# One pass for the row maximum and the row factor in layer 1's softmax, and slots that return when a store has landed

## The chip, the cores and the metric

The kernel runs on one core of a Trainium2 chip. The metric is the device time of one execution in microseconds, as the median of several runs. The profile of a kernel is one execution, taken by the hardware profiler.

## What is computed

Two layers, each an attention and a feed-forward part. Every part is wrapped the same way: `x = x + LN(part(LN(x)))`. x is (2, 512, 512) in float32. Layer 0's attention is causal with 32 query heads and 8 key heads; layer 1's attention, where the change lies, has 32 heads of 128 and normalizes queries and keys by their root mean square:

```
q = rmsnorm(x @ Wq + bq, gq); k = rmsnorm(x @ Wk + bk, gk); v = x @ Wv + bv
scores = einsum('bnhd,bmhd->bhnm', q, k) / sqrt(128)
attn = softmax(scores)
out = einsum('bhnm,bmhd->bnhd', attn, v) @ Wo + bo
rmsnorm(x, w) = w * (x * rsqrt(mean(x*x) + 1e-6))
```

The feed-forward parts are a linear layer with low-rank additions (layer 0), and a gated one with 1376 hidden columns and low-rank additions (layer 1).

## The kernel before, in words

**Precision and tiles.** Products are kept near float32 by splitting each operand into a rounded high half and the rest, and adding three products (`mm3`, line 393). The high half is a rounding copy, mostly on ScalarE; the low half is a difference on GpSimd or VectorE. The 512 rows of each batch element are four tiles of 128 rows. Activations stay transposed in SBUF (`xh`, `xl`), the sums of a part in `y`.

**Units.** A layer's attention is cut into 16 head pairs for 2 batch elements, 32 units per layer. In layer 1 a unit projects K and Q (`proj`, line 1039), squares and sums them for the root mean square, and takes the power -0.5 on GpSimd; for K the factor is multiplied in, for Q it is kept as `rq`, one column for each tile and head (line 1084), and applied to the scores. K is multiplied by `g`, the product of the two weight vectors and 1/sqrt(128) (`consts`, line 429). In most units the transposes are made in 32x32 blocks on VectorE and put in place by a trip through DRAM (`flip`, line 1097, buffers kdk and kdq); in a layer's first and last units TensorE transposes.

**The scores.** `l1_score` (line 1169) issues, for each tile of 128 queries, three products of 512 columns into a PSUM bank, then on VectorE the negated row maximum `m` of the bank (line 1178), then the product `mr = m * r` with the row's factor r from `rq`, another VectorE instruction on 128x1. `softmax_tail` (line 681) follows: ScalarE takes `exp(r * s + mr)` from the bank and its row sums, VectorE the reciprocal, one of three engines multiplies the rows by it; then VectorE transposes blocks, DMA writes them to DRAM (pd) and reads them back in place, and each piece is split and used in the product with V (`av_items`, line 839). Layer 0's scores (`l0_score`, line 989) get their causal mask and row minimum in one VectorE pass over the bank, in place, and an exponential with scale -1 and bias m.

**The order of the work.** Python writes the program in the order of a plan that it makes while it runs. Every stage is a generator; `yield` hands the stage back to the planner until the planner's clocks say that what it has issued is done. `Engine.cost` (line 70) prices each instruction: on VectorE a 512-wide pass over PSUM at 512/960 + 0.07 us, the same for a row maximum and for a scaling; on ScalarE every row operand of the scale, the bias or the sum adds 0.093 us. `pick` (line 127) gives an operation to the engine that would be done first. `streams` (line 345) interleaves the units: scores and V products in main order, projections and output products as fills. Each engine executes its instructions in the order in which they were written, so the plan fixes each queue. All transfers are issued on SP's queue.

**Slots.** A tile is taken from a slot and given back with `rel` when its last reader is issued. The large tiles are halves of 37 shared slots; `NBUF` and `PHASES` (line 40) cap how many each kind may have. The hardware still makes the next writer of a slot wait for the reader.

**The residual.** `resid` (line 549) forms x + LN(y) for a tile; `store` (line 580) adds the row constant in a tile `xo` from the slots "A", writes it to DRAM (xd) on SP's queue and gives the slot back right there (line 590); the last level writes the output and gives back x in the same way (line 573).

Of the kernel before, what the change touches and what calls it, by code (L numbers as in the profile page):

```python
# [14 lines left out]
ALU = mybir.AluOpType  # L15
AX = mybir.AxisListType
# [40 lines left out]
class Item:  # L57
    """a piece of TensorE's work, to be issued when cond holds"""

# [4 lines left out]
class Engine:  # L64
    """An engine that keeps its order of issue, with a clock (us) of its work."""

# [57 lines left out]
class Engines:  # L124
    WEIGHT = dict(vector=1.0, scalar=0.5, gpsimd=0.0)

    def pick(self, *cands):
        """issue the one of the candidates (engine, op, args...) that is done first"""
        def score(x):
            e = getattr(self, x[0])  # L130
            kw = x[-1] if isinstance(x[-1], dict) else {}
            c = e.cost(x[1], [y for y in x[2:] if not isinstance(y, dict)], kw)
            t = max(e.free, e.k.now + LAT)
            for y in x[2:]:
                if isinstance(y, bass.AP) and y.space == PSUM:
                    t = max(t, e.k.banks.get(y.name, 0.0))
            return t + c * (1 + self.WEIGHT[x[0]])
        x = min(cands, key=score)
        kw = x[-1] if isinstance(x[-1], dict) else {}
        return getattr(getattr(self, x[0]), x[1])(*[y for y in x[2:] if not isinstance(y, dict)], **kw)  # L140
# [9 lines left out]
    def mul(self, out, a, s):  # L150
        """by a factor of each row"""
        self.pick(("gpsimd", "tensor_scalar", out, a, s, 1.0, ALU.mult, ALU.mult),
                  ("vector", "tensor_scalar", out, a, s, None, ALU.mult),
                  ("scalar", "activation", out, a, AF.Copy, dict(scale=s)))

    def copy(self, out, a):
        """from PSUM"""
        self.pick(("scalar", "copy", out, a), ("vector", "tensor_copy", out, a))
# [8 lines left out]
class Kern:  # L167
    """Work is written as items: functions, or generators that yield the time
    (of TensorE's work) after which their next stage is to be issued."""

# [30 lines left out]

# [1 line left out]
    def slot(self, tag):  # L203
# [12 lines left out]

    # the large tiles: a half or the whole of a slot each (halves of one type only in a slot)
    HALF = dict(W=2, Wk=1, nat=2, v=2, PT=2, TN=2, KT=2, raw=1, bb=1, bqk=1, qk=1, P=1, x=1, A=1, T=1, xn=1, pt=1, ot=1,
# [52 lines left out]

# [1 line left out]
    def step(self, g):  # L273
# [22 lines left out]
    def phase(self, i):  # L296
        """what is tuned for each phase of the work"""
        for k, v in PHASES[i].items():
            if k in self.NBUF:
                self.NBUF[k] = v  # L300
            elif k in self.nc.WEIGHT:
                self.nc.WEIGHT[k] = v
            else:
                setattr(self, k, v)
# [20 lines left out]
    def wait(self, tag, n=1):  # L325
        """in a stage: until n slots are free, first come first served"""
        q = self.queues.setdefault(tag, [])
        ticket = object()
        q.append(ticket)
        while q[0] is not ticket or not self.has(tag, n):  # L330
            yield 0.1
        q.pop(0)

    def low(self, eng):
        """in a stage of low priority: until the engine has nothing issued to it"""
        e = getattr(self.nc, eng)
        while e.free > self.now + 0.01:
            yield e.free - self.now
# [6 lines left out]
    def streams(self, main, fills, bg):  # L345
        """Issue the streams of items, each in its order: a fill when its nominal place in
        main has come, or main waits; bg starts at its nominal place."""
        mi = bi = idle = 0
# [27 lines left out]

# [1 line left out]
    def pe(self, t):  # L378
        """t: at the full clock, which TensorE has after a busy tick only"""
        s = max(self.clk, self.now)  # L380
# [12 lines left out]
    def mm3(self, out, pairs, start=True, stop=True):  # L393
        """exact hi/lo products: hi hi + hi lo + lo hi"""
        n = len(pairs)
# [8 lines left out]

# [1 line left out]
    def setup(self):  # L406
# [22 lines left out]
    def consts(self):  # L429
# [4 lines left out]
        yield  # L434
        nc.vector.scalar_tensor_tensor(self.g, self.gqk[:, 0:1], SCALE, self.gqk[:, 1:2], ALU.mult, ALU.mult)

# [3 lines left out]

# [1 line left out]
    def split(self, hi, lo, raw):  # L442
        """hi + lo = raw exactly"""
        nc = self.nc
# [33 lines left out]

# [1 line left out]
    def ln_stats(self, src):  # L480
# [68 lines left out]
    def resid(self, b, tt, lvl):  # L549
        """x of level lvl + 1 = x + LN(y); returned short of a constant of each row"""  # L550
        nc = self.nc
# [9 lines left out]
        if lvl == 3:  # L561
# [9 lines left out]
            yield  # L571
            nc.sync.dma_start(self.xsrc(b, tt, 4), x)
            self.rel(x)
            return
# [5 lines left out]
        def store():  # L580
# [5 lines left out]
            if lvl == 0:  # L586
                self.xin[b, tt, 1] = xo
                return
            nc.sync.dma_start(self.xsrc(b, tt, lvl + 1), xo)
            self.rel(xo)  # L590
        self.spawn(store)
        return x

    def boundary(self, b, tt, lvl):
        """from the finished y of level lvl on"""
        x = yield from self.resid(b, tt, lvl)
# [18 lines left out]

# [1 line left out]
    def out_proj(self, b, first, last, ot, w, badd, lvl):  # L617
        """y += O Wo over the heads of this unit"""
        def one(tt):
# [61 lines left out]
    def softmax_tail(self, st, j, qt, ps, bias, scale, w):  # L681
# [13 lines left out]
        if not st.get("lag"):  # L695
            st["p", j, qt] = pr
            return
        # P^T = 32 x 32 blocks transposed on VectorE, and the blocks put in place on their way through DRAM
        yield from self.wait("T")
# [60 lines left out]
    def unit_done(self, st):  # L760
        """after the last use of V"""
        if st["vlast"]:
            self.rel(*st["v"]["v"])
            if "v32" in st["v"]:
                self.rel(st["v"]["v32"])

    def pv_items(self, st, j, voff, causal, bias):
        """transposes of P, then O^T = V^T P^T, split"""
        box = {}
# [69 lines left out]
    def av_items(self, st, j, voff, bias):  # L839
        """O^T = V^T P^T by halves of the queries, split"""  # L840
        box = {}
# [41 lines left out]

# [1 line left out]
    def l0_init(self):  # L885
# [11 lines left out]
    def l0_zero(self):  # L897
        """the parts of pd0 that stay unused"""
        nc = self.nc
# [113 lines left out]

# [1 line left out]
    def l1_init(self):  # L1015
# [18 lines left out]
    def l1_pre(self, hp, b, w, lag):  # L1034
# [62 lines left out]
        def flip(n):  # L1097
            """the transposes as 32 x 32 blocks on VectorE, put in place on their way through DRAM"""
            nat = st["nat" + n]
# [69 lines left out]
    def l1_score(self, st, j):  # L1169
        def one(qt):  # L1170
# [4 lines left out]
            if qt == NT - 1:  # L1175
                self.rel(*st["q"][j], *st["k"][j])
            m = self.t("m", [P, 1])
            nc.vector.tensor_reduce(m, ps, AX.X, ALU.max, negate=True)
            yield
            while "rq" not in st:  # L1180
                yield 0.3
            r = st["rq"][:, 2 * qt + j:2 * qt + j + 1]
            mr = self.t("mr", [P, 1])
            nc.vector.tensor_tensor(mr, m, r, ALU.mult)
            yield
            self.rel(m)
            yield from self.softmax_tail(st, j, qt, ps, mr, r, S)
            if j and qt == NT - 1:
# [3 lines left out]

# [1 line left out]
    def f0_init(self):  # L1194
# [38 lines left out]

# [1 line left out]
    def f1_init(self):  # L1235
        """rows 0:16, 32:48, 64:80 of the pieces: hi of a low-rank factor, lo in block k; others 0"""
        nc, a = self.nc, self.a
# [150 lines left out]
    def f1_post(self, js, b, sts, last):  # L1388
        """y += g W2 over the chunks of units js"""
        def one(tt):  # L1390
# [29 lines left out]

# [1 line left out]
    def run(self, nu0=16, nu1=16, nf=6):  # L1422
        # at the ends of a layer's units some run batch by batch, each then with weights of its own
        units = []
# [17 lines left out]
        def pre(n):  # L1442
            """early, mid items and state of unit n"""
            if n not in sts:
# [43 lines left out]
        for k in FIRST.split():  # L1488
            for f in todo[k]:
                self.do(f)  # L1490
        # weights start this many units before (early, mid, late parts)
        bgs = {}
# [143 lines left out]
def _layout(i):  # L1636
    """Layouts of the arrays only: transposes and tilings."""
    n = {k: np.asarray(v) for k, v in i.items()}
# [44 lines left out]
```

## Time and profile before

| | us |
|---|---|
| median of 3 runs | 2111.77 (2107.32 to 2115.55) |
| span of the profiled execution | 2117.8 |
| TensorE busy | 2056.7 |
| VectorE busy | 1801.4 |
| GpSimd busy | 1446.3 |
| ScalarE busy | 1337.7 |

The span is the profiled execution's own time, from its first to its last instruction; it lies 0.3% above the median of the runs. In the lines below, PE is TensorE's products and PEld its weight loads, DVE is VectorE, ACT is ScalarE, POOL is GpSimd, SP the engine that issues transfers. A group names the tiles that are written and read (`m<-ps_s`), without their numbers: ps_s is a bank of scores, ps_pj of projections, ps_oy of V products and output products, ps_tr of transposes; `ar` is any large tile of the shared slots. Every instruction has line L102, since a helper records them all; groups are told apart by tiles and shapes. A number after a bar is busy time, then the mean duration of one in ns, then the idle time of the engine just before them and what ended it. "PEclk" is the granted clock of TensorE as a share of the full one.

Layer 1's attention begins at about 750 us (its first rq at 754.4) and its last exponential is issued at 1896.2.

### The profile page before, as it was taken

To read this page: it belongs to the slowest core of one execution; us is meant where nothing else is said; L and a number is where in the kernel's file an instruction comes from. 1 tells how busy PE (TensorE), PEld (TensorE's weight loads), DVE (VectorE), ACT (ScalarE), POOL (GpSimd) and SP (SyncE) were. 2 spreads that over 40 slices of the span, in tenths; PEclk is the share of its full clock that TensorE was granted. 3 is DMA by queue.
4 is the path that set the end of the run, shared out by engine and by line. 5 is a ranking of instruction groups with operands and counts; after the bars stand their busy time and mean duration, and the time that the engine had idled before them with its cause. 6 is when DMAs were issued, how large, how long until landed. Compare 5 with 4: busy or idle time off the path is not lost.

```text
span 2117.8 us, 41211 instructions
## 1 busy us (share of the span) xinstructions
PE 2056.7 (97%) x12605; PEld 1827.5 (86%) x12605; DVE 1801.4 (85%) x4210; ACT 1337.7 (63%) x3247; POOL 1446.3 (68%) x1786
## 2 busy tenths in 40 slices
PE   8999999999999999999999999999999999989998
PEld 7888888888888798889899999999999898977886
DVE  7998899899888889889889999899989988888534
ACT  5776677577766668776666666666667666664212
POOL 5686678688875567877677777777777776774212
PEclk9999999999999999999999999999999999999999
DMA  2476567577652235887877777777777787763021
GB/s 98 127 183 166 145 185 183 143 200 199 177 159 66 71 103 166 244 232 223 227 202 229 220 227 211 207 221 219 225 206 232 213 240 212 224 178 93 31 67 44
DMA packets 476566, 370.54 MB, mean 175 GB/s; under 512 B 117400, under 2 KB 424488, under 8 KB 476344
## 3 DMA queue, kind: packets, MB, share of 16 engines
q1 hardware_dynamic: 476344, 367.91, 60.9%
q8 instruction: 99, 1.62, 0.3%
q14 instruction: 123, 1.01, 0.2%
HBM read 232.12 MB, written 135.66 MB: 174 GB/s over the span
## 4 chain that ended last, share of the span: by engine, by line
PE 54%; DMA 12%; DVE 9%; SPq 3%; issue 2%; POOL 2%; ACT 2%; DVEq 0%; ACTq 0%; POOLq 0%
PE ps_pj L102 23%; PE ps_oy L102 19%; PE ps_s L102 10%; DVE ar L102 6%; SPq L102 3%; DMA pd<-ar 3%; DMA ar<-pd 2%; POOL ar L102 2%; DMA kdk<-ar 2%; ACT ar L102 2%; DMA ar<-kdq 2%; DMA kdq<-ar 2%; PE ps_tr L102 1%; DMA ar<-pc 1%; DVE m L102 1%
## 5 line engine op out<-in xcount | busy, mean ns | idle before, releaser
L102 POOL TENSOR_TENSOR ar<-ar,ar 128x256 fp32r<-128x256 f32 (+4 forms) x1223 | 1058.3, 887 | 456.6 <-ACT ar L102 333.6
L102 PE MATMUL ps_oy<-ar,ar 128*128 128x256 f32 (+2 forms) x4014 | 832.2, 342 | 28.7 <-DVE ar L102 14.0
L102 PEld LDWEIGHTS ps_oy<-ar,ar 128*128 128x128 f32 x4014 | 653.5, 190 | 133.1 <-DVE ar L102 22.5
L102 ACT CAST ar<-ar 128x256 fp32r<-128x256 f32 (+3 forms) x1166 | 531.5, 490 | 305.4 <-DMA ar<-pd 117.1
L102 PE MATMUL ps_pj<-ar,xh 128*128 128x256 f32 (+1 forms) x3392 | 635.2, 285 | 0.9 <-POOL ar L102 0.6
L102 PEld LDWEIGHTS ps_pj<-ar,xh 128*128 128x128 f32 x3392 | 536.0, 190 | 14.5 <-POOL ar L102 1.1
L102 PE MATMUL ps_pj<-ar,xl 128*128 128x256 f32 (+1 forms) x1696 | 482.9, 285 | 0.0
L102 DVE STREAM_TRANSPOSE ar<-ar 128x256 f32<-128x256 f32 (+3 forms) x688 | 347.9, 533 | 16.9 <-DMA pd<-ar 9.7
L102 DVE TENSOR_TENSOR ar<-ps_pj,ar 128x512 f32<-128x512 f32 (+2 forms) x448 | 305.4, 683 | 52.5 <-PE ps_pj L102 44.8
L102 PE MATMUL ps_s<-ar,ar 128*128 128x512 f32 (+2 forms) x1252 | 338.5, 376 | 8.6 <-DVE ar L102 4.7
L102 PEld LDWEIGHTS ps_pj<-ar,xl 128*128 128x128 f32 x1696 | 322.9, 190 | 2.1 <-DVE xl L102 0.7
L102 PE MATMUL ps_pj<-xh,ar 128*128 128x512 f32 x816 | 286.6, 399 | 0.7 <-ACT xh L102 0.7
L102 DVE TENSOR_TENSOR y<-ps_oy,y 128x512 f32<-128x512 f32 x272 | 184.8, 680 | 81.8 <-PE ps_oy L102 80.2
L102 PEld LDWEIGHTS ps_s<-ar,ar 128*128 128x128 f32 x1252 | 214.5, 189 | 44.0 <-DVE ar L102 12.6
L102 DVE TENSOR_TENSOR ar<-ar,ar 128x256 fp32r<-128x256 f32 (+5 forms) x328 | 207.9, 652 | 51.1 <-ACT ar L102 50.1
L102 ACT ACTIVATE ar<-ps_s,mr,rq 128x512 f32<-128x512 f32 x256 | 198.6, 777 | 46.7 <-DVE mr L102 36.9
L102 PEld LDWEIGHTS ps_pj<-xh,ar 128*128 128x128 f32 x816 | 154.0, 189 | 31.7 <-ACT xh L102 1.1
L102 DVE TENSOR_REDUCE m<-ps_s 128x1 f32<-128x512 f32 x256 | 170.9, 673 | 6.2 <-PE ps_s L102 5.0
L102 ACT ACTIVATE ar<-ar,ri 128x512 f32<-128x512 f32 (+3 forms) x245 | 149.6, 621 | 38.3 <-DVE ri L102 37.1
L102 POOL TENSOR_SCALAR ar<-ar,ri 128x512 f32<-128x512 f32 (+3 forms) x202 | 133.0, 661 | 54.3 <-DVE ri L102 48.9
L102 PE MATMUL ps_pj<-xl,ar 128*128 128x512 f32 (+1 forms) x408 | 161.2, 395 | 0.0
L102 ACT ACTIVATE ar<-ps_s,m 128x512 f32<-128x512 f32 (+3 forms) x256 | 133.8, 526 | 23.4 <-DVE m L102 14.8
(91 smaller groups left out, 2105.5 us busy)
## 6 DMA issues: line engine op xcount, KB each, us to landing
pd<-ar SPq DMA_DIRECT2D x240, 256.0 KB, 3.7
ar<-pd SPq DMA_DIRECT2D x480, 128.0 KB, 3.3
ar<-pc SPq DMA_DIRECT2D x200, 128.0 KB, 3.0
ar<-in_wq SPq DMA_DIRECT2D x86, 256.0 KB, 4.1
ar<-in_wo SPq DMA_DIRECT2D x86, 256.0 KB, 3.6
kdk<-ar SPq DMA_DIRECT2D x31, 512.0 KB, 4.8
ar<-kdk SPq DMA_DIRECT2D x124, 128.0 KB, 4.0
kdq<-ar SPq DMA_DIRECT2D x31, 512.0 KB, 5.1
```

What stands on the lines that cost most here:

```text
L102: r = self.k.tc.keep_in_program_order(f(*args, **kw))
```

## The change

In layer 1 the row maximum and its multiplication by the factor become one VectorE pass over the bank: it multiplies every score by the row's factor in place, and its accumulator output is the row's minimum. `g` gets a minus sign, so the bank holds negated scores and the minimum is the negated maximum. The exponential gets the constant scale -1 and the bias m, as in layer 0. The pass is written behind the wait for `rq`, which in the kernel before stood between the maximum and the product. The residual's slots are given back one stage later, when the planner has the store as landed. The rest of the diff removes comments.

```diff
@@ consts
-        nc.vector.scalar_tensor_tensor(self.g, self.gqk[:, 0:1], SCALE, self.gqk[:, 1:2], ALU.mult, ALU.mult)
+        nc.vector.scalar_tensor_tensor(self.g, self.gqk[:, 0:1], -SCALE, self.gqk[:, 1:2], ALU.mult, ALU.mult)
@@ resid, the last level
             nc.sync.dma_start(self.xsrc(b, tt, 4), x)
+            yield
             self.rel(x)
@@ resid, store
             nc.sync.dma_start(self.xsrc(b, tt, lvl + 1), xo)
+            yield
             self.rel(xo)
@@ l1_score
-            m = self.t("m", [P, 1])
-            nc.vector.tensor_reduce(m, ps, AX.X, ALU.max, negate=True)
-            yield
             while "rq" not in st:
                 yield 0.3
             r = st["rq"][:, 2 * qt + j:2 * qt + j + 1]
-            mr = self.t("mr", [P, 1])
-            nc.vector.tensor_tensor(mr, m, r, ALU.mult)
+            m = self.t("m", [P, 1])
+
+            nc.vector.tensor_scalar(ps, ps, r, 3.0e38, ALU.mult, ALU.min, accum_out=m)
             yield
-            self.rel(m)
-            yield from self.softmax_tail(st, j, qt, ps, mr, r, S)
+            yield from self.softmax_tail(st, j, qt, ps, m, -1.0, S)
```

## The prediction

> **What bounds the kernel now.** I read the page's busy line first, then the busy time by stage, then what TensorE waits for in each stage, then the groups of instructions with their shapes kept apart.
>
> The page:
>
> ```profile
> PE 2056.7 (97%) x12605; PEld 1827.5 (86%) x12605; DVE 1801.4 (85%) x4210; ACT 1337.7 (63%) x3247; POOL 1446.3 (68%) x1786
> ```
>
> TensorE is busy 97% of the span, VectorE 85%. A busy TensorE need not be TensorE at its pace, so I looked at the chain that ended last: twelve products of 256 columns take 1.42 us wherever they follow each other (0.118 us each), twelve of 512 take 2.78 (0.232 each), early, late and in the middle. That is its pace, and the change touches no product. Hence the stages (my cuts: layer 0; the way to layer 1; its first units; its steady part; its last units; the feed-forward):
>
> ```profile
> core 0: us, PE busy (x) PEld busy (x) DVE busy (x) ACT busy (x) POOL busy (x), PEclk, DMA share, GB/s
> 0.00:640.00 640.00, 624.18 (x3408) 543.35 (x3409) 559.71 (x1480) 435.02 (x1227) 469.28 (x570) 1.00 0.60 163
> 640.00:780.00 140.00, 136.50 (x809) 116.12 (x808) 120.67 (x302) 86.84 (x202) 81.98 (x120) 1.00 0.21 69
> 780.00:1100.00 320.00, 307.99 (x2064) 279.02 (x2064) 282.68 (x624) 227.97 (x511) 241.28 (x291) 0.99 0.75 217
> 1100.00:1700.00 600.00, 595.26 (x4184) 552.45 (x4183) 547.03 (x1213) 390.61 (x901) 448.90 (x544) 1.00 0.76 219
> 1700.00:1910.00 210.00, 195.76 (x1263) 177.11 (x1262) 177.31 (x396) 140.46 (x309) 150.55 (x187) 0.96 0.74 211
> 1910.00:2118.00 208.00, 197.00 (x884) 159.48 (x882) 114.01 (x199) 56.78 (x101) 54.28 (x75) 0.99 0.18 58
> ```
>
> The second number is the length, the third TensorE's busy time. In the steady part TensorE lacks 4.7 us of 600: nothing there can bring much. It lacks 12.0 us in the first units and 14.2 in the last, and there the granted clock dips too: 0.01 x 320 = 3.2 us and 0.04 x 210 = 8.4. Layer 1's attention thus has 15.2 + 4.7 + 22.6 = 42.5 us to give, all that this change can win there. What TensorE waits for, first in the steady part, then in the last units (us, times, longest):
>
> ```profile
> PE ps_s L102 <- DVE ar L102: 4.2, 13, 0.5
> PE ps_oy L102 <- DVE ar L102: 0.4, 1, 0.4
> ```
>
> ```profile
> PE ps_oy L102 <- POOL ar L102: 5.6, 8, 1.5
> PE ps_oy L102 <- DVE ar L102: 3.6, 3, 2.2
> PE ps_tr L102 <- ACT ar L102: 2.5, 2, 1.6
> PE ps_oy L102 <- ACT ar L102: 2.2, 3, 1.5
> ```
>
> In the steady part it is VectorE alone, by tenths of a us. At the end it is whichever engine prepares the split probabilities for the product with V: a long chain that the order of issue placed too close.
>
> **The change part by part.** The rows that price it (busy us, mean ns of one):
>
> ```profile
> L102 ACT ACTIVATE ar<-ps_s,mr,rq 128x512 f32<-128x512 f32 x256 | 198.6, 777 | 46.7 <-DVE mr L102 36.9 <-DVE ri L102 4.1 <-DVE ar L102 2.1
> L102 DVE TENSOR_REDUCE m<-ps_s 128x1 f32<-128x512 f32 x256 | 170.9, 673 | 6.2 <-PE ps_s L102 5.0
> L102 DVE TENSOR_TENSOR mr<-m,rq 128x1 f32<-128x1 f32 x256 | 92.2, 365 | 0.0
> L102 DVE CUSTOM_DVE_ANT_0 ps_s<-ps_s,ar 128x512 f32<-128x512 f32 x64 | 44.8, 700 | 0.7 <-PE ps_s L102 0.6
> L102 ACT ACTIVATE ar<-ps_s,m 128x512 f32<-128x512 f32 x64 | 43.9, 686 | 4.6 <-DVE m L102 4.6
> L102 DVE DVE_READ_ACCUMULATOR2_ANT m<- 128x1 f32 x256 | 35.1, 137 | 0.0
> ```
>
> *VectorE, removed:* 256 x (673 + 365) = 265.7 us. *Added:* 256 passes that read a bank of scores, write it back and leave a row minimum. No such form is in the trace. The nearest is layer 0's masked pass, same tile and shape, also in place: 700 ns, and 137 for the reading of its accumulator. Ends: one instruction without a read-out at 669 (the scaling by a row factor in SBUF, 128x512), and 853 + 137 (the slowest 512-wide row, a product-and-sum over SBUF). The sums are -94, -51.5 and -12 us; I take -51.5. None is a loss.
>
> [...] The row says 365 for the tiny product, with 107 to 2451 ns from fastest to slowest. [...] The trace's mean decides: it is what VectorE's queue lost. [...]
>
> *ScalarE:* the constant scale takes 777 to 686 ns: 256 x 91 = -23.3 us. The score's chain gets shorter by some 0.3 us.
>
> *What the order of issue moves* (both programs compared, counts by form): 18 of the 128x1024 multiplications by g go from GpSimd (1.19 us) to ScalarE (1.15); row factors 16 from GpSimd, 7 from VectorE to ScalarE; 36 of the 256-wide roundings from ScalarE to VectorE, 12 of the 512-wide back; 21 of the 256-wide differences to GpSimd, 27 of the 512-wide ones to VectorE. With their mean durations: VectorE -45 us in all, ScalarE +5, GpSimd -52. Layer 1's attention (780 to 1910) has VectorE busy 1007 of 1130 us, 89%; it becomes 85%. No engine becomes a bound. Products (12,473) and transfers (2,098) stay the same in number.
>
> *The steady part* stays at TensorE's pace; of its 4.7 us I give back a third, -1.5.
>
> *First and last units:* here the order counts. I counted, in both orders, TensorE's work (at 0.118 and 0.234 us a product) between a head's scores and the product with V that uses them. First units: before, 10 of 14 such distances are under 27 us (down to 19.0); after, 4 of 10 (down to 18.5). Last units: the shortest goes from 18.8 to 20.2; from scores to a transpose on TensorE from 6.4 to 9.2. In the steady part 31.3 becomes 28.4 in half the units: still long. So I give back half of the first units' 15.2 (-7.5) and somewhat under a quarter of the last units' 22.6 (-5).
>
> *Slots given back at landing:* xo (16 stores) and the output tiles (8) stay taken for the 2.0 to 6.5 us of a landing. Cover: 74 half slots, and other work on ScalarE. What it removes is seen: ScalarE waited 3.4 us in 3 places for such stores, off the path. Without cover a writer waits a landing, as it did. Zero; ends -3.4 and +6.5. Where they stand on SP's queue, loads follow them; none waits newly there. The sign in g: zero, one 128x1 instruction either way.
>
> *A new wait:* the pass needs the row factor, so VectorE may stand at it with everything queued behind: sums into y (which hold TensorE's banks), transposes, split differences. See the third case.
>
> Sum: -1.5 - 7.5 - 5 = -14 us of the profiled 2117.8 (its span; nothing beyond it is counted). The runs' median is 2111.77, 0.3% below; scaled, 2098.
>
> **The rivals.** *Hidden anyway:* VectorE isn't the bound, the steady part is full, and the stalls at both ends belong to the chain through DRAM (3.7 us out, 3.3 in), which the change leaves. Then only 1.5 us and some 2 at the ends are won: 2108. For it: DMA and TensorE carry most of the chain there. Against it: the distances that got longer.
>
> *Slower, by the row factor:* GpSimd makes it (1.65 us) once per unit of 35 us. Between it and its first reader lay at least 11.2 us of TensorE's work before; in the new order 6.3 at least, in many units. It decides once GpSimd runs more than 6 us behind. If TensorE then loses 1.5 us in each of 16 units, 24 us: 2136. Against it: GpSimd waits 333.6 us for ScalarE in total, so it is mostly early; no wait of VectorE for the factor is in the trace.
>
> *All recovered:* 42.5 us, 2069; no reason why every stall should go.
>
> **How the numbers follow.** Forecast (stalls at the ends shrink) 45%, around 2098, its own range 2086 to 2101; hidden 35%, 2102 to 2116; slower by the factor or an equally unlucky order 17%; more than forecast 3%. A measurement tells about 0.5%, 10.6 us, from no change: below 2101.2 is faster, above 2122.3 slower. The unknown pass (-94 to -12 on VectorE) moves the result by a few us through the same stalls. For 8 in 10 the range is 2082 to 2121.
>
> **What would show it.** The pass as two rows near 700 and 137 ns, no mr row, the exponential at 686; VectorE about 45 us less busy; TensorE's idle time between 780 and 1100 near 6 us and its clock dips fewer; the steady part's at 3 to 4. Wrong if VectorE waits at the pass for rq, if the pass costs over 1 us, or if TensorE's waits at ps_oy in the first or last units are no smaller.

## The result

| | median us | lowest to highest | runs |
|---|---|---|---|
| before | 2111.80 | 2107.32 to 2115.55 | 5 |
| after | 2120.33 | 2117.39 to 2127.33 | 5 |

The changed kernel takes 1.0052 times as long as the kernel before, with a 95% interval of 1.0031 to 1.0072: slower by about 11 us by the ratio (8.5 by the medians of the table). The forecast was 2098 us. The range given (2082 to 2121) just holds the median; its direction is the other one. Later ratios are all to the kernel before, run beside it on the same chip. That kernel's own median lies between 2107.8 and 2115.0 us in the five later sessions, so only ratios are compared. Between sessions a ratio can move by more than its interval: one kernel, run in two of them, gave 1.0015 and 1.0035. Differences of 0.1 or 0.2% between runs of different sessions are therefore read with care.

### The profile page after: what moved, and what is told of

Read it like the earlier page. It is cut to its first block, busy times and chain, and to the rows that moved or that the text cites. A ratio compares the mean times of both kernels' runs of the same rounds, so it can differ in the third digit from the quotient of the medians.

```text
span 2118.5 us, 41177 instructions
## 1 busy us (share of the span) xinstructions
PE 2055.8 (97%) x12605; PEld 1828.2 (86%) x12605; DVE 1760.9 (83%) x4236; ACT 1347.8 (64%) x3260; POOL 1408.0 (66%) x1747
## 5 line engine op out<-in xcount | busy, mean ns | idle before, releaser
L102 POOL TENSOR_TENSOR ar<-ar,ar 128x256 fp32r<-128x256 f32 (+3 forms) x1217 | 1041.7, 879 | 475.2 <-ACT ar L102 351.2
L102 ACT CAST ar<-ar 128x256 fp32r<-128x256 f32 (+2 forms) x1142 | 529.8, 494 | 277.3 <-PE ps_oy L102 78.8
L102 DVE STREAM_TRANSPOSE ar<-ar 128x256 f32<-128x256 f32 (+3 forms) x688 | 348.3, 534 | 14.9 <-DMA pd<-ar 8.6
L102 PE MATMUL ps_s<-ar,ar 128*128 128x512 f32 (+2 forms) x1304 | 345.2, 378 | 11.5 <-ACT ar L102 6.7
L102 ACT ACTIVATE ar<-ps_s,m 128x512 f32<-128x512 f32 (+3 forms) x512 | 309.7, 607 | 58.1 <-DVE ps_s L102 25.1
L102 PEld LDWEIGHTS ps_s<-ar,ar 128*128 128x128 f32 x1304 | 221.4, 189 | 48.7 <-ACT ar L102 10.9
L102 DVE TENSOR_TENSOR ar<-ar,ar 128x256 fp32r<-128x256 f32 (+5 forms) x334 | 217.1, 667 | 53.0 <-ACT ar L102 48.2
L102 DVE TENSOR_SCALAR_CACHE_REDUCE ps_s<-ps_s,rq 128x512 f32<-128x512 f32 x256 | 188.9, 743 | 9.6 <-PE ps_s L102 9.3
L102 ACT ACTIVATE ar<-ar,ri 128x512 f32<-128x512 f32 (+3 forms) x268 | 166.5, 632 | 46.5 <-DVE ri L102 45.7
L102 POOL TENSOR_SCALAR ar<-ar,ri 128x512 f32<-128x512 f32 (+3 forms) x186 | 125.5, 677 | 70.4 <-DVE ri L102 62.8
L102 DVE CUSTOM_DVE_ANT_0 ps_s<-ps_s,ar 128x512 f32<-128x512 f32 (+3 forms) x256 | 121.5, 488 | 4.5 <-PE ps_s L102 4.0
```

Source lines behind the costliest of these rows:

```text
L102: r = self.k.tc.keep_in_program_order(f(*args, **kw))
```

## The profile after

The busy line of the page answers to the one shown first for before:

```profile
PE 2055.8 (97%) x12605; PEld 1828.2 (86%) x12605; DVE 1760.9 (83%) x4236; ACT 1347.8 (64%) x3260; POOL 1408.0 (66%) x1747
```

VectorE lost 40.5 us of work, as forecast to within 5. ScalarE gained 10 us (forecast: 5), though its exponentials became cheaper (777 to 687 ns), and GpSimd lost 38 (forecast: 52). The relief of VectorE was real; part of it went to ScalarE, to which the new plan hands more work.

The rows of the new softmax, with shapes kept apart (busy us, mean ns of one, then idle time before them and what ended it):

```profile
L102 DVE TENSOR_SCALAR_CACHE_REDUCE ps_s<-ps_s,rq 128x512 f32<-128x512 f32 x256 | 188.9, 743 | 9.6 <-PE ps_s L102 9.3
L102 DVE DVE_READ_ACCUMULATOR ps_s<-ps_s,rq 128x1 f32 x256 | 35.3, 138 | 0.0
L102 ACT ACTIVATE ar<-ps_s,m 128x512 f32<-128x512 f32 x320 | 219.6, 687 | 39.3 <-DVE ps_s L102 25.1 <-DVE ri L102 6.4 <-DVE m L102 3.9
```

The pass costs 743 + 138 = 881 ns where 673 + 365 = 1038 stood. What it waits for is the scores (9.3 of 9.6 us), not `rq`. The exponential is at 687. So each instruction did what it was meant to do.

The busy time by stage, in the same cuts:

```profile
core 0: us, PE busy (x) PEld busy (x) DVE busy (x) ACT busy (x) POOL busy (x), PEclk, DMA share, GB/s
0.00:640.00 640.00, 627.84 (x3424) 546.64 (x3425) 562.31 (x1487) 437.00 (x1232) 470.84 (x571) 1.00 0.60 163
640.00:780.00 140.00, 136.75 (x809) 116.26 (x808) 120.28 (x303) 88.14 (x203) 84.64 (x124) 1.00 0.22 71
780.00:1100.00 320.00, 307.09 (x2077) 280.96 (x2076) 272.76 (x636) 223.96 (x509) 234.37 (x280) 0.98 0.76 219
1100.00:1700.00 600.00, 597.20 (x4200) 554.71 (x4199) 518.31 (x1225) 407.14 (x921) 419.64 (x520) 1.00 0.75 220
1700.00:1910.00 210.00, 193.17 (x1239) 172.60 (x1239) 178.49 (x396) 136.60 (x301) 145.46 (x179) 0.97 0.72 206
1910.00:2118.00 208.00, 193.76 (x865) 157.03 (x864) 108.75 (x193) 55.01 (x97) 53.02 (x76) 0.98 0.17 55
```

TensorE's idle time in the first units is 12.9 us (12.0 before): nothing given back there. In the steady part it is 2.8 (4.7). In the last two stages it rose, from 14.2 to 16.8 and from 11.0 to 14.2. The two profiled spans (2117.8 and 2118.5) hide the loss: layer 0, whose code is the same, had done 3408 products by 640 us in the one execution and 3424 in the other. A single execution of this kernel moves by several us, so the stages only say where to look; the verdicts below come from timed runs.

What TensorE waits for in the changed kernel's last stage, and below it the same in the kernel before (us in total, times, longest):

```profile
PE ps_tr L102 <- ACT ar L102: 4.0, 2, 2.2
PE ps_oy L102 <- DVE ar L102: 1.1, 1, 1.1
```

```profile
PE ps_tr L102 <- ACT ar L102: 0.6, 1, 0.6
PE ps_oy L102 <- DVE ar L102: 0.5, 1, 0.5
```

Two waits of about 2 us stand where 0.6 stood. They are at the transposes of the layer norm, on the passage from layer 1's attention to the feed-forward, a place that the prediction did not look at.

## Experiments

The runs are numbered e1 to e18, in the order in which their expectations stand; every ratio is from five rounds, with 5 to 22 executions of the kernel named.

### Instructions and order taken apart

The plan is made from the planner's prices, so the two can be separated. In the first run the planner charges its clocks for the instructions that were removed while the new ones are written:

```diff
+            nc.vector.tensor_scalar(ps, ps, r, 3.0e38, ALU.mult, ALU.min, accum_out=mn)
+            yield
...
+            v.free = max(v.free, self.now + LAT) + 1 / 960 + 0.07
...
+            yield from self.softmax_tail(st, j, qt, ps, mn, -1.0, S, 0.093)
```

By the traces, TensorE's, GpSimd's and SP's queues are then those of before, instruction by instruction, and VectorE's and ScalarE's too but for the replaced ones. The second run does the reverse, in the changed kernel's queues: maximum and product are written, but charged as the one pass, with ScalarE charged 0.093 us less.

> Layer 1's new instructions (one pass, constant scale) in the order of issue of the kernel before: the planner is charged for the removed instruction and for the dearer exponential, so that TensorE's, GpSimd's and SP's queues are those of before, instruction by instruction, and VectorE's and ScalarE's too but for the replaced ones. Theory ORDER (the new instructions are cheaper and the new order of issue loses more than they win): 2103 to 2110 us, 2 to 8 us below the kernel before. Theory INSTRUCTION (the pass in place, or its wait for the row factor, costs TensorE time): 2117 to 2123, like the changed kernel.

> The converse: the row maximum, the product with the factor and the exponential with two row operands, in the order of issue of the changed kernel (the planner is charged as for the one pass). Theory ORDER: 2120 to 2130, no faster than the changed kernel and slower than before. Theory INSTRUCTION: about 2112, like before.

Measured: new instructions in the old order 0.9985 (0.9974 to 0.9997), in a repetition on another chip 0.9992 (0.9981 to 1.0003, told below); old instructions in the new order 1.0134 (1.0114 to 1.0155). So the instructions are worth a little, 0.1%, in the old order, and 0.8% in the new one (1.0134 to 1.0052); and the new order costs 0.6% with the new instructions (1.0052 less 0.9989, the mean of the two), 1.3% with the old. The 0.8 and the 0.6% compare runs of two sessions, but they are three times what the repetition of one kernel moved, or more. The order is what loses. For the old instructions it loses more than the 2120 to 2130 us that ORDER expected (1.0134 of 2112 is 2140).

### Which part of the diff changes the order

The third run has only the score part of the diff, the fourth only the two `yield`s ahead of `rel(x)` and `rel(xo)`.

> The score's part of the change alone, planned freely; the residual's slots are given back as before. If the score's part makes the loss: 2116 to 2124. If the slots do: 2100 to 2112. By theory ORDER any free plan may land anywhere within some 10 us of before, so that score part and slot part need not add up to the whole.

> The residual's slots given back at the landing, alone; the scores as before. Its instructions are those of before, only in another order. If only instructions matter: 2112, no difference. Theory ORDER: a difference of 3 to 10 us from before, of either sign, though nothing that runs has changed.

Measured: scores only 1.0043 (1.0031 to 1.0055), slots only 0.9995 (0.9983 to 1.0007). Alone, the slots do nothing: by the traces every engine keeps its order of instructions, so the difference of 3 to 10 us that ORDER expected for e4 had no ground. Together with the score's part they do change the plan. TensorE's queue in e3 is the changed kernel's for its first 11,598 of 12,605 instructions and then another, in which this is all that TensorE waits for from 1910 us on:

```profile
PE ps_oy L102 <- DVE ar L102: 0.2, 1, 0.2
```

The two waits of 2 us are not there, and e3 is still slower than the kernel before by 0.43%. So they cannot be all of the loss.

### The passage to the feed-forward

Layer 1's last 24 output products finish the rows of the last batch element. Before a row tile can be transposed for the feed-forward, it goes through the sum into y, the row statistics, the factor and a second layer norm, over VectorE, GpSimd and ScalarE. In the kernel before, two feed-forward blocks of 12 products (into ps_s and ps_pj) come behind the 24; in the changed kernel they come ahead of them. The expectations below speak of the blocks as lying between the last products into `ps_oy`; by the traces they lie behind layer 1's output products, among the feed-forward's own products into `ps_oy`.

TensorE's timeline of the kernel before, without the lines of the two blocks, which fill 1938.6 to 1941.4 and 1944.7 to 1947.5 (start, us, instructions, then idle time and its releaser in brackets):

```profile
1931.69 7.11 PE L102 MATMUL ps_oy<-ar,ar 128*128 128x512 f32 x30
...
1941.42 1.54 PE L102 MATMUL ps_oy<-ar,ar 128*128 128x512 f32 x6
1942.80 0.64 PE L102 MATMUL ps_tr<-ar,ar 96*128 96x256 f32 x4
1943.28 1.58 PE L102 MATMUL ps_oy<-ar,ar 128*128 128x512 f32 x6
...
1947.45 1.54 PE L102 MATMUL ps_oy<-ar,ar 128*128 128x512 f32 x6
1949.61 0.66 PE L102 MATMUL ps_tr<-ident,ar 128*128 128x128 f32 x4 [0.62 <-ACT ar L102]
```

And of the changed kernel, complete:

```profile
1933.25 9.92 PE L102 MATMUL ps_oy<-ar,ar 128*128 128x512 f32 x42
1943.01 0.64 PE L102 MATMUL ps_tr<-ar,ar 96*128 96x256 f32 x4
1943.48 2.96 PE L102 MATMUL ps_oy<-ar,ar 128*128 128x512 f32 x12
1948.67 0.66 PE L102 MATMUL ps_tr<-ident,ar 128*128 128x128 f32 x4 [2.23 <-ACT ar L102]
1951.13 1.12 PE L102 MATMUL ps_tr<-ident,ar 128*128 128x128 f32 x4 [1.80 <-ACT ar L102]
1951.89 4.01 PE L102 MATMUL ps_oy<-ar,ar 128*128 128x512 f32 x12
```

The sum of the first row tile starts on VectorE at 1933.27 in the first and at 1934.84 in the second. From there to the transposes with `ident` it is 16.3 and 13.8 us, and TensorE has work for 15.7 and for 11.6 of them. The chain is not slower in the changed kernel; it has lost its cover, the work that TensorE has meanwhile. A second cost follows: the last twelve products take 4.01 us where twelve take 2.96 three rows above. The granted clock of the changed kernel says why:

```profile
core 0: us, PE busy (x) PEld busy (x) DVE busy (x) ACT busy (x) POOL busy (x), PEclk, DMA share, GB/s
1940.00:1950.00 10.00, 7.09 (x34) 5.39 (x32) 9.68 (x23) 3.72 (x6) 5.26 (x11) 1.00 0.20 79
1950.00:1960.00 10.00, 8.87 (x39) 7.43 (x40) 6.96 (x15) 5.20 (x9) 4.79 (x8) 0.83 0.08 29
```

VectorE is busy 9.68 of 10 us in the stretch with the first hole, which suggests that the chain can hardly go faster there; in the next stretch the clock is 0.83, worth 1.7 us of 10. With the 4.0 us of waits that is some 6 us.

The fifth run mends only this: in the changed kernel the two blocks are held until one and two row tiles have their last output products issued, which puts them where they were before. The sixth spoils it in the kernel before: the output products are held until nine blocks are issued.

```diff
 # the changed kernel, blocks behind            (f1_pre)
-Item(lambda n=n: ok(n), ...)
+Item(lambda n=n: ok(n) and self.lp >= {7: 1, 8: 2}.get(self.ff, 0), ...)
 # the kernel before, blocks ahead              (run, post(NA - 1))
+y.cond = lambda ok=y.cond: ok() and self.ff >= 9
```

Here `ff` counts the blocks issued and `lp` the row tiles whose last output products are issued. Away from this place TensorE's queue stays as it was.

> The changed kernel, with one edit to its plan: the last two feed-forward blocks of 12 products that it issued ahead of layer 1's last output products are held until one and two of those output products are issued, which is the order of the kernel before at this place; all else of the plan stays. Theory BOUNDARY (the changed kernel loses at the passage from layer 1's attention to the feed-forward, since its last output products run back to back and the layer norm of their rows has nothing left to hide behind): TensorE's waits at ps_tr for ScalarE from 1910 us on go from 4.0 to under 1.5 us, and the time falls by 4 to 8 us, to some 2114 (ratio to the kernel before 1.0000 to 1.0033). Rival PLAN ELSEWHERE (the loss sits in the stages of layer 1's attention, whose order differs too): the time stays within 2 us of the changed kernel, ratio 1.004 to 1.007.

> The kernel before with the opposite edit: its last output products of layer 1 are held until nine feed-forward blocks are issued, so that they run back to back as in the changed kernel; instructions of the same kinds, all else of the plan stays. Theory BOUNDARY: slower than the kernel before by 4 to 8 us (ratio 1.002 to 1.004), with new waits of TensorE at ps_tr for ScalarE of 3 to 5 us after 1910. Rival PLAN ELSEWHERE: within 2 us, ratio 0.999 to 1.001.

Measured: changed kernel with the blocks behind 1.0017 (1.0007 to 1.0027), 0.35% less than without (measured in another session); kernel before with the blocks ahead 1.0028 (1.0018 to 1.0037), 0.28% more. In the traces, the two waits at ps_tr for ScalarE come to 0.7 us in the first, and to 4.0 in the second. Both directions agree: the passage costs 6 to 7 us. The traces say so too. TensorE's last 783 instructions are the same set in these four kernels and take 176.5 us in the kernel before, 183.3 in e6, 181.1 in the changed kernel and 177.4 in e5. The rival PLAN ELSEWHERE falls for this part, but not as a whole: 1.0017 is still 0.3% above 0.9989.

### Other plans

Two more plans of the changed kernel: K's multiplication by g fixed on GpSimd (which the changed plan had moved to ScalarE, 18 times), and another planner constant.

```diff
-                nc.mul(kt, kt, self.g)
+                nc.gpsimd.tensor_scalar(kt, kt, self.g, 1.0, ALU.mult, ALU.mult)
 # the other run
-LAT = 0.1
+LAT = 0.12
```

> The changed kernel with K's multiplication by g fixed on GpSimd, where nearly all of it stood in the kernel before, instead of left to the planner's choice (which moved 18 of them to ScalarE). The plan made around it differs in layer 1, keeps the two feed-forward blocks between the last output products, and has the longest distances of all between scores and V product. BOUNDARY: 2103 to 2112, near the new instructions in the order of before (2109). Rival LUCKY PLAN (the plan of the kernel before is well matched to the chip as a whole and any new one loses some 10 us somewhere): 2117 to 2128.

> The changed kernel with the planner's constant for the latency from one engine to the next at 0.12 us instead of 0.10: the same instructions in another plan, which like the changed kernel runs the last output products back to back (shortest distances from output product to the transposes of its rows 7.0 to 12.5 us of TensorE's work). BOUNDARY: 2116 to 2128, as slow as the changed kernel or slower. If it comes below 2112, back-to-back output products do not decide.

Measured: g on GpSimd 1.0041 (1.0028 to 1.0054), constant 0.12 1.0070 (1.0049 to 1.0091). The second is as BOUNDARY expected, but says little: its queue leaves the others' at TensorE's 155th instruction, in layer 0, and it waits 11.3 us in the steady part as well. The first is a miss for BOUNDARY and lies where LUCKY PLAN put it. With the blocks behind and the longest distances that I had counted, it still loses 0.5% against 0.9989. So the passage is not all, distances between scores and V product do not foretell the time, and the 18 multiplications on ScalarE are not the whole cause either.

### Where the rest lies

A plan is made forward in time, so one can be changed from a given tile of scores on. Ahead of each tile the planner's pricing is chosen by the number of tiles issued, 256 in all; the instructions are the new ones throughout. The expectations call e10 "new plan later" and e13 "new plan steady only".

```diff
+            self.sc = getattr(self, "sc", 0) + 1
+            if self.sc <= 48:      # e10; > 48 in e9; not in range(49, 177) in e13;
+                ...                # <= 208 in e14; <= 192 in e15: priced as the removed instructions
+            else:
+                ...                # priced as the changed kernel does
```

> The new instructions throughout. For the first 48 of layer 1's 256 tiles of scores the planner prices them as the changed kernel does, for the other 208 as the removed ones: TensorE's queue is that of the changed kernel up to 45% of its instructions, and that of the new instructions in the order of before over its last 55%. What is left of the changed kernel's loss once the passage to the feed-forward is mended is 0.32% (1.0017 against 0.9985). FIRST UNITS (this rest was lost in the first units): ratio near 1.0017. LATER (it was lost in the steady part and the last units): near 0.9985, as the new instructions in the order of before. In shares: in between.

> The new instructions throughout, the other way round: the first 48 tiles of scores priced as the removed ones, the rest as in the changed kernel. TensorE's queue is that of the order of before up to 45%, then a plan close to the changed kernel's, with the last output products back to back (42 in a row). FIRST UNITS: 0.9985 plus 0.0035 for the passage, 1.002. LATER: as the changed kernel, 1.005.

> The kernel of the run ahead of this one, with the two feed-forward blocks held until one and two of the last output products are issued. BOUNDARY, confirmed a second time if this is 0.0025 to 0.0035 below that run. FIRST UNITS: 0.9985, all of the loss undone. LATER: 1.0017.

> The new instructions in the order of before, a second time, as the yardstick for the three runs beside it on the same chip: 0.9974 to 0.9997 if the first measurement (0.9985) holds, at or above 1.0000 if its gain was chance.

> The new instructions throughout; the planner prices tiles of scores 49 to 176 of 256 as the changed kernel does, and all others as the removed instructions. TensorE's queue is that of the order of before in its first 45% and its last 19%, and that of the plan of the run new plan later in between, up to 76%. STEADY (the rest of the loss, some 0.3 to 0.45%, is lost in the steady part, by many small waits): ratio 1.001 to 1.004. LAST UNITS (it is lost after the steady part): 0.998 to 1.000, as the new instructions in the order of before. The trace should say the same: in the stages after 1000 us the scores' products come later by some 6 us in all (STEADY) or not at all.

> The new instructions throughout; the planner prices the first 208 tiles of scores as the removed instructions, and the last 48 as the changed kernel does: TensorE's queue is that of the order of before in its first 83%. At the passage to the feed-forward this plan keeps the two blocks between the last output products (30, block, 6, block). STEADY: 0.998 to 1.000. LAST UNITS: 1.001 to 1.004.

> As the run ahead of this one, but with the first 192 tiles priced as the removed instructions, 64 as in the changed kernel: TensorE's queue is that of the order of before in its first 79%, and here the plan runs the last 42 output products back to back. BOUNDARY: slower than the run ahead of it by 0.13 to 0.35%, with waits of TensorE at ps_tr for ScalarE of some 4 us at the passage; if the two are equal, the passage alone costs nothing.

| new plan in | ratio | 95% interval |
|---|---|---|
| nowhere (e1) | 0.9985 | 0.9974 to 0.9997 |
| nowhere, again (e12) | 0.9992 | 0.9981 to 1.0003 |
| first units (e9) | 0.9987 | 0.9978 to 0.9997 |
| steady part (e13) | 1.0015 | 1.0003 to 1.0026 |
| steady part, again (e18, told below) | 1.0035 | 1.0025 to 1.0045 |
| last units, blocks behind (e14) | 0.9987 | 0.9978 to 0.9996 |
| last units, blocks ahead (e15) | 1.0031 | 1.0021 to 1.0042 |
| all from the steady part on, blocks ahead (e10) | 1.0049 | 1.0032 to 1.0067 |
| the same, blocks behind (e11) | 1.0036 | 1.0022 to 1.0050 |
| everywhere (the changed kernel) | 1.0052 | 1.0031 to 1.0072 |

The first units and the last units, taken alone, neither lose nor gain. The steady part loses 0.26% and, in the repetition, 0.46% against 0.9989: 0.36% in the mean, some 7.6 us. The repetition, 1.0035, lies outside the 1.0003 to 1.0026 expected of it; only its sign repeats. The passage costs 0.13 to 0.44% in its four pairs (e11 to e10, before to e6, e5 to after, e14 to e15). The smallest of them, 0.13%, is below the 0.25 that BOUNDARY expected at least, and its intervals overlap; the largest is above the 0.35 expected at most and also has 16 more tiles in the new plan. e11 itself, at 1.0036, missed the 1.0017 that LATER gave it. With the mean of the four, 0.30%, the sum is 0.36 + 0.30 = 0.66%, and 0.63% are to be explained (1.0052 less 0.9989). That the two meet so closely is luck: the shares are uncertain by 0.1% or more, and e3 loses 0.43% without the passage.

The traces of single executions point the same way. TensorE's instructions 5,727 to 10,255 are the same set in all kernels named here. In the order of before they take 646.0 to 651.9 us (e1, e9, e12, e14), in the new plan 658.3 and 655.9 (e13, e18), some 8 us more; e13 had expected some 6.

Where the steady part loses is not to be seen at one place. TensorE's waits from 1000 to 1600 us with the new plan in the steady part (e13), and below in the order of before with the same instructions (e12):

```profile
PE ps_s L102 <- ACT ar L102: 3.7, 6, 1.5
PE ps_s L102 <- DVE ar L102: 2.0, 3, 1.2
PE ps_s L102 <- POOL ar L102: 1.8, 3, 1.0
PE ps_oy L102 <- DVE ar L102: 1.7, 2, 1.5
```

```profile
PE ps_s L102 <- DVE ar L102: 2.1, 7, 0.5
PE ps_oy L102 <- DVE ar L102: 0.7, 1, 0.7
```

9.2 us of waits stand against 2.8, but this sum does not part the two orders: it is 5.5 in e1, the same program as e12, 6.4 in the kernel before and 6.0 in the changed one. What is new is the scores' wait for ScalarE. With the order of before it is at most 0.4 us in any run, with the new plans told so far 1.8 to 6.6 (e8, with 0.3, is the exception). ScalarE's rounding copies of 512 columns, from 1000 to 1600 us, show what it waited for itself, again in e13 and then in e12:

```profile
L102 ACT CAST ar<-ar 128x512 fp32r<-128x512 f32 x132 | 80.0, 616 | 32.9 <-DMA ar<-kdq 14.7 <-DMA ar<-in_wv 6.1 <-DMA ar<-in_wo 4.2
```

```profile
L102 ACT CAST ar<-ar 128x512 fp32r<-128x512 f32 x126 | 74.3, 616 | 9.1 <-DMA ar<-in_wo 4.5 <-DVE ar L102 2.1 <-DMA ar<-kdq 1.2
```

14.7 us of idle time were ended by Q's blocks coming back from DRAM (`kdq`), against 1.2. One case of e13's timeline, ScalarE and then TensorE:

```profile
1434.32 0.62 ACT L102 CAST ar<-ar 128x512 fp32r<-128x512 f32 x1 [2.25 <-DMA ar<-kdq]
```

```profile
1434.99 1.91 PE L102 MATMUL ps_s<-ar,ar 128*128 128x512 f32 x6 [0.81 <-ACT ar L102]
```

The loads of these blocks are issued from 1428.71 on; the high half of Q is made the moment that they have landed, and the scores start the moment that it is made. A load takes 3.8 us from issue to landing in the median, and 3.7 in e12: it is not slower, it is issued too close ahead of its scores. ScalarE is not overloaded there, it waits. The same number parts all kernels told so far. With the order of before in the steady part these copies wait for kdq 0.9 to 1.5 us (3.7 in the slots-only kernel, under 1.1 in e14); with the new ones told so far it is 11.4 to 20.1 (13.9 in the changed kernel, 20.1 with g on GpSimd).

That is an agreement of traces. Two of three last runs try it (the third repeats e13): in the plan, Q's blocks are taken as landed later than before, so that more work goes between their loads and their scores.

```diff
 # flip, behind the four loads
             yield
+            if n == "q" and 48 < getattr(self, "sc", 0) <= 176:   # e16; in e17 1.5 and no upper end
+                yield 1.0
             if n == "k":
```

> The kernel of the run new plan steady only, with one edit: from tile of scores 49 to 176 the planner takes Q's blocks as landed 1.0 us later than it did, so that it puts more work between their loads from DRAM and the scores that use them. TensorE's first 45% and last 21% are again those of the order of before. Theory Q LATE (the steady part loses because Q's blocks come back from DRAM too close ahead of their scores): ScalarE's idle time ended by kdq in its 512-wide copies from 1000 to 1600 us falls from 14.7 to under 5, TensorE's waits there from 9.2 to some 4, and the ratio from 1.0015 to 0.999. Rival ANY NEW ORDER (the late blocks are a by-product): the kdq idle time falls, the ratio stays at 1.001 to 1.002.

> The kernel of the run new plan later with blocks between, with 1.5 us more for Q's blocks from tile 49 to the end: the changed kernel's prices in the steady and the last units, both faults mended. Q LATE: 0.998 to 1.000, against 1.0036 without this edit. ANY NEW ORDER: 1.002 to 1.005.

> The run new plan steady only a second time, as the yardstick beside the two others on the same chip: 1.0003 to 1.0026 if its first measurement (1.0015) holds; at 0.999 if the steady part's loss was chance.

Measured: e16 0.9995 (0.9984 to 1.0006), e18 beside it 1.0035 (1.0025 to 1.0045), e17 1.0067 (1.0052 to 1.0083). ScalarE's copies and then TensorE's waits of e16, 1000 to 1600 us:

```profile
L102 ACT CAST ar<-ar 128x512 fp32r<-128x512 f32 x136 | 82.9, 617 | 31.3 <-DMA ar<-in_wv 11.7 <-DMA ar<-kdq 5.3 <-PE ps_pj L102 4.2
```

```profile
PE ps_s L102 <- POOL ar L102: 2.8, 4, 0.9
PE ps_oy L102 <- DVE ar L102: 1.9, 2, 1.6
PE ps_oy L102 <- POOL ar L102: 0.5, 2, 0.4
PE ps_s L102 <- DVE ar L102: 0.4, 1, 0.4
PE ps_s L102 <- ACT ar L102: 0.3, 1, 0.3
```

The wait for kdq fell from 14.7 (14.9 in e18) to 5.3, the scores' wait for ScalarE from 3.7 to 0.3, and the time by 0.40% against e18, beside it on the same chip. The waits in all fell to 5.9 us, not to the 4 expected. One price in the plan, 1 us more, takes the steady part's loss away: instructions 5,727 to 10,255 take 651.3 us, as in the order of before. It does so without going back to that order, from which TensorE's queue in e16 differs in 392 places (in e13, 316). Weights that come late are not what e13 lost by: ScalarE's wait for them (in_wv) rose from 6.1 to 11.7 us. In this plan, then, Q LATE holds. But the edit also draws a new plan for the whole steady part, and e17 is a miss for both theories, above the 1.005 of ANY NEW ORDER. There kdq is down to 5.0 too, and yet TensorE waits more from 1000 to 1600 us than in e13, 10.9 us, now mostly for VectorE and GpSimd (its lines have L103, since the helper stands one line further down):

```profile
PE ps_oy L103 <- DVE ar L103: 5.7, 5, 1.4
PE ps_s L103 <- POOL ar L103: 4.7, 6, 1.5
```

In the last units TensorE lacks 19.4 us of 210 from 1700 to 1910 (16.8 in the changed kernel), at a clock of 0.95. So late Q blocks are one way for a plan to lose in the steady part, the one that e13 shows; that they are all of the changed kernel's loss there is not shown. Mending one fault of a plan draws a new plan behind it.

At the passage, e14 and e15 repeat what the changed kernel showed. In e14 the wait at these transposes is 0.65 us. In e15:

```profile
1928.19 9.95 PE L102 MATMUL ps_oy<-ar,ar 128*128 128x512 f32 x42
...
1943.61 0.66 PE L102 MATMUL ps_tr<-ident,ar 128*128 128x128 f32 x4 [2.20 <-ACT ar L102]
1946.08 1.12 PE L102 MATMUL ps_tr<-ident,ar 128*128 128x128 f32 x4 [1.81 <-ACT ar L102]
1946.84 5.45 PE L102 MATMUL ps_oy<-ar,ar 128*128 128x512 f32 x12
```

The clock in e15 is 0.77 from 1940 to 1950 and 0.89 in the next 10 us, in e14 1.00 in both.

A part of the losses is the clock's. In the timed runs its mean is 0.9942 to 0.9947 for the kernel before in every later session, 0.9943 in e16, 0.9935 in e18, 0.9920 in the changed kernel and 0.9896 in e2. As an estimate, 0.0025 of 2118 us is 5 of the changed kernel's 11 us. At its passage this is seen: the two waits cost their own 4.0 us, and from within the second one on the clock was half for 3.41 us (last section).

The best versions are the new instructions in an order close to that of before: e1, e9 and e14, each about 0.1% under the kernel before, some 2 to 3 us. The repetition e12, at 0.9992, has an interval that reaches 1.0003, so this gain is small and barely shown.

## Why the prediction was wrong

**The bound** held: TensorE is busy 97% of the span in the kernel before, in the changed kernel and in e1, and 96% in e2, and no other engine became one.

**The pass** was taken at 700 + 137 and measured 743 + 138, within its bounds. The instructions alone were put at -51.5 us; by the rows they are 256 x (881 - 1038) = -40, and with the order held VectorE is busy 31 us less (1801.4 to 1770.2 in e1). With the new order the -45 came out as -40.5. To take the tiny product at its mean in the trace, 365 ns, though its fastest took 107, was right for VectorE's time: in e2, which has it still, its mean was 346. What makes it so long was not shown.

**ScalarE's** 91 ns per exponential are there (777 to 687; 1337.7 to 1314.8 us in e1). That the order of issue hands it more than this, +5 in all, was forecast; it became +10.

**The steady part** (-1.5) was a miss in sign. With the order held nothing is lost there; in the new plan of e13 it costs 5.5 to 9.7 us (0.26 and 0.46%), which goes when Q's trip through DRAM is planned 1 us longer (e16). I had named transfers through DRAM only in a rival, for both ends, as something that the change leaves alone. I had also reasoned that it runs at TensorE's pace and cannot move much, which bounds what can be won there but not what can be lost.

**First and last units** (-7.5 and -5, nearly all of the forecast gain) are the steps that failed. They rested on two distances in the order, scores to V product and scores to transposes, which grew. Taken alone, the new plan in the first units brings nothing against the same instructions in the old order (0.9987 against 0.9989), and neither does that in the last units (0.9987). So these distances, as counted, are not what sets the time of these stages. The signs named for them did not come: TensorE's idle time from 780 to 1100 us is 12.9 us, not near 6, and its clock 0.98, not above 0.99. I had not counted a third distance, from a row tile's last output product to the transposes of its layer norm: for the first row tile of the last batch element it fell from 15.7 to 11.6 us of TensorE's work. It was in the compared orders to be read, and is worth the 6 to 7 us of e5 and e6. So the sum failed where it took gains in these units from a longer cover, and where it put the losses of a new order, 13 us in all, at nothing.

**The slots** at zero: right when alone (0.9995). With the score's part they move the plan of the passage, which the zero did not think of. **The wait for the row factor**: right to be set aside; no wait of VectorE for it is in the trace after.

**The rivals.** "Hidden anyway" had the instructions right: it put their worth at 3.5 us, and in the order of before they bring 2 to 3. "Slower" happened, but not by the row factor: by what its case called an equally unlucky order, which was named without a place or a price. The sum gave the order credit for gains and no debit.

## What to carry to other kernels

Where a planner or scheduler makes the order, a cheaper instruction is two changes: its own time, which here was worth 2 to 3 us, and a new order everywhere behind it, which here cost 13. Take them apart by letting the planner charge the old prices for the new instructions, and keep the old order if it is the better one. When orders are compared, list, for every place where the bounding engine meets a long chain of the others (a trip through DRAM, a layer norm), how much of its work covers that chain, the passages between phases first. The two losses found here were a chain of 14 to 16 us whose cover fell by 4, and, in e13's plan, a load issued less than 6 us ahead of its use. And time a repaired plan anew: e17 had both repaired and, at 1.0067, was no faster than the changed kernel.

## What the runs showed of the hardware

A VectorE pass of 128x512 over a PSUM bank that multiplies by a row factor in place and leaves the row minimum takes 743 ns in the changed kernel, and reading the minimum is a second instruction of 138. TensorE's work has two holes of 2.23 and 1.80 us at the passage of the changed kernel. Within the second the clock fell to half for 3.41 us, so they cost twice. Three stretches around that (columns as in the busy time by stage; the clock is the third number from the end):

```profile
1947.21:1950.62 3.41, 0.66 (x4) 0.42 (x4) 3.34 (x8) 2.77 (x5) 1.94 (x5) 1.00 0.21 79
1950.62:1954.03 3.41, 2.90 (x9) 2.52 (x10) 3.31 (x8) 2.82 (x5) 2.52 (x5) 0.50 0.22 78
1954.03:1957.44 3.41, 3.41 (x18) 2.79 (x18) 2.20 (x5) 1.13 (x3) 1.64 (x4) 1.00 0.01 4
```

TensorE worked 0.66 of 3.41 us, and its clock was half for the next 3.41; the last 12 products took 4.01 us where 12 take 2.96. In e15 the clock around the same two waits (2.20 and 1.81 us) is 0.77 in the mean from 1940 to 1950 us and 0.89 in the next 10 us: as an estimate, (2.3 + 1.1) / 0.5 = 6.8 us at half the clock. The 12 products behind them took 5.45 us, 12 ahead of them 2.95. So the same two holes cost up to 1.7 us by the clock in one execution and, by this estimate, up to 3.4 in the other. The 3.41 us ahead of the lower clock were not idle throughout: the longest hole of the changed kernel's passage was 2.2 us, with 0.66 us of work before the next. In the traces of the kernel before and of the changed kernel, their start and end aside, there are six and seven stretches at half the clock; each lasts 3.41 or 6.83 us, and TensorE was busy for at most 54% of the 3.41 us ahead of it. Not every hole has one behind it: in the changed kernel TensorE stood still for 1.81 us from 973.3 us on, and the clock from 973 to 985 is 1.00.
